# The last 16 channels in eight PSUM banks, and one set of statistics inside the first product group

## The chip, the cores and the metric

One core of a Trainium2 chip runs the kernel. TensorE (PE) multiplies, VectorE (DVE), ScalarE (ACT) and GpSimd (POOL) do the element work, SyncE (SP) issues most of the DMAs. The metric is the device time of one execution in microseconds.

## What is computed

A ConvNeXt block on 32 images of 384 channels and 28 x 28 positions in float32, followed by a channel gate:

```python
y = conv7x7_depthwise(x) + dw_b                 # per channel
mu, var = mean(y, channels), var(y, channels)   # per position
y = (y - mu) * rsqrt(var + EPS) * ln_g + ln_b
y = gelu(y @ w1 + b1)                           # 384 -> 1536
gx = sqrt(sum(y * y, positions)); nx = gx / (mean(gx, features) + EPS)
y = grn_g * (y * nx) + grn_b + y
x = x + (y @ w2 + b2)                           # 1536 -> 384
avg, mx, mn = mean(x, positions), max(x, positions), min(x, positions)
logits = concat(avg @ W1.T, grouped(mx, W2_1) * W2_2, mn @ W3.T) @ Wfc.T
out = sigmoid(logits + x)
```

## The kernel before

*The convolution.* Channels go in 48 steps `s` of eight, four pairs a step. For each channel, three matmuls (L697, L699, L701) multiply the turned image rows of all images by a banded matrix `tmat`. The result of a pair stands in one PSUM bank `pc`. VectorE turns it into `yt` (L704) and adds it to `acc`, the sum over channels (L712). ScalarE squares `yt` into `sq` (L718), and POOL adds the squares of two pairs to `ssum` (L728). Each `yt` of eight channels is stored to the scratch tensor `yd`.

*The last 16 channels.* They are done in step 47, in two halves of images (0 to 15, then 16 to 31), so that image 0 is ready earlier. The four banks `pc_half` serve eight pairs in turn. Each half adds its own share to `acc` and to its own copy of `ssum`, and is stored to `yd`: the first in whole tiles, the second in quarters from SP's and ScalarE's queues. Between the halves, image 0's last 16 channels are read back from `yd` (`load_y_part`).

*The statistics.* `finish` runs twice, once for each half of the images: mean, variance, square root, reciprocal, and a store of the reciprocal `rs` to the scratch tensor `rsd`. Its temporary tiles (`late`) lie in a buffer of the convolution's `xt` pool. From `rsd`, `load_rb(b)` brings the factors of one image to all partitions as `rb`.

*Forms.* A 3 x 6 block of operands (three channel blocks, two halves of the positions) is multiplied by a 3 x 3 block of weights with 15 products instead of 18. The operands are the forms p to x and z, made of sums of the blocks `0a` to `2b` (`FORMS`, made in `forms_up`), and three of the blocks themselves. The weights of the 15 products, `u1d`, are made during the convolution. For image 0, whose factors come too late, the products work on data that is not yet multiplied by `rs`. Its result is multiplied afterwards (`stretch`, L944). Forms q, t and u of image 0 are made by POOL before the last step, and the rest by VectorE after it (`first_image(2)`).

*The up-projection.* `up(b, hooks)` computes y for image b in two groups of two tiles each (`t2` is 0, then 2). A group runs the 15 steps of `UPSTEPS`, each for both tiles. A step is one product into a bank (A, B or C of its tile), after which the listed reads are done: a copy by ScalarE, or additions by VectorE. A bank that is written anew waits until it has been read. Weights are loaded by `load_u1` in portions of five steps into six rotating buffers in `ws`. After each product `run(hooks, (t2, step))` issues other work that was entered for that place: a step's number is twice the row's number, plus one for the second tile.

*What the hooks hold.* `within(b)` enters work for `up(b)`: for image 0 the normalization of image 1 (`normed`) and its forms, the stretches and gelu of image 0, and the loads of image 2's y (`load_y`); for image 1 the rest of image 0's work (stretch, gelu, `square`, `grn`, `scale`) and the sums of its down-projection. `beside(b)` does the same for `down(b)`.

*The down-projection.* `down(b)` runs 38 steps of six matmuls on 39 `SUMS` of y. A sum of 128 x 588 elements is one POOL instruction (L1069) into a slot of `d_room`, into a place that has become free, or over an operand that is not used again.

*Order.* A scheduler orders each engine's instructions at build time. `keep_in_program_order` puts an instruction behind the one traced before it on its engine; DMAs that SP issues count as SP's instructions. An engine runs its list in order, so one that waits holds up what stands behind it. Memory of the convolution's pools is given to later pools (`up2`, `tep`, `yp`, `xp`, `d_room`), which wait for its last readers. `before` runs `load_rb(0)`, `load_y(1)`, `up(0)`, `up(1)`, `down(0)`, then `up(2)`, `down(1)`, and so on.

Of the kernel before, what the change touches and what calls it, by code (L numbers as in the profile page):

```python
# [13 lines left out]
P = 128  # L14
# [72 lines left out]
)  # L87
NS = len(UPSTEPS)
KT = FB // 3
# [108 lines left out]
def convnext_gate_kernel(  # L198
# [24 lines left out]
    rsd = [dram.tile([P, YR], F32, name=f"rsd_{i}") for i in range(2)]  # L223
# [18 lines left out]
    fct = const.tile([P, CB, NQ, R], F32, name="fct")  # L242
    eps_t = const.tile([P, 1], F32, name="eps_t")
# [9 lines left out]
    def load_u1(t, i):  # L253
        n = len(u1_tiles) % NU1
        w = ws[:, n * UG * P : (n + 1) * UG * P].rearrange("p (g c) -> p g c", c=P)
        nc.sync.dma_start(w, u1d[t, :, i : i + UG, :])
        u1_tiles.append(w)
        return w
# [23 lines left out]
    def load_rb(b):  # L282
        if b == 0:
            rb = d_room[:, : NQD * YR].rearrange("p (q n) -> p q n", n=YR)
        else:
            rb = rbp.tile([P, NQD, YR], F32, tag="rb", name=f"rb_{b}")
        rbs[b] = rb
        base = rsd[0 if b < B0 else 1]
# [3 lines left out]
                tensor=base.tensor,  # L292
                offset=base.offset + b * YR,
# [4 lines left out]
    def load_y_part(b, yi, cb, p0, p1):  # L298
        nc.sync.dma_start(
            yi[p0:p1, cb],  # L300
            yd.rearrange("(q b) c n -> b c q n", b=B)[b, cb * P + p0 : cb * P + p1],
        )
# [25 lines left out]
    def forms_up(b, eng=nc.gpsimd, early=None):  # L328

        if b in feats:  # L330
            o, af = feats[b], early_af.pop()
            make_forms(b, eng, o, af, [d for d in FORMS if d[0] not in EARLY])
            return
        acc = accs.pop(b)
        o = feats[b] = {
            f"{k}{'ab'[h]}": acc[:, k, h * NH : (h + 1) * NH] for k in range(CB) for h in range(2)
        }
        ns = len(FORMS) - 1
        if b == 1:

            n = -(-ns * NH // (KD * NQ4))
            reserved.extend(slots[SLOTS - n :])
            del slots[SLOTS - n :]
            aft = d_room[:, (SLOTS - n) * KD * NQ4 :]
            af = [aft[:, n * NH : (n + 1) * NH] for n in range(ns)]
        else:
            af = [room_af[:, n, :] for n in range(ns)]
        if early:
            early_af.append(af)
        make_forms(b, eng, o, af, [d for d in FORMS if not early or d[0] in EARLY])  # L350

    EARLY, early_af = ("q", "t", "u"), []

    def make_forms(b, eng, o, af, todo):
        places = [d[0] for d in FORMS if d[0] != "w"]
        for name, place, in0, in1, op in todo:
            d = o[place] if name == "w" else af[places.index(name)]
            tc.keep_in_program_order(eng.tensor_tensor(d, o[in0], o[in1], op))  # L358
            o[name] = d


    with ExitStack() as one:
# [8 lines left out]
        finp = one.enter_context(tc.tile_pool(name="finp", bufs=1))  # L371
# [70 lines left out]
        ssum = finp.tile([P, SQ, YR], F32, name="ssum")  # L442
        acc = finp.tile([P, 2, N], F32, name="acc")
        dws = finp.tile([P, 1], F32, name="dws")
        lr = tp.tile([P, CB, 2], F32, name="lr")
        mcol = tp.tile([P, FB], F32, name="mcol")
        for t in (ssum, acc):
            nc.gpsimd.memset(t, 0.0)
# [224 lines left out]
        def conv(s, c2, yt, xt, b0, b1):  # L673
# [7 lines left out]
            else:  # L681

                pc = pcs.pop(0)
                pcs.append(pc)
# [21 lines left out]
            def part(v):  # L706
                if nb == B:
                    return v
                return v.rearrange("p c (j b) -> p c j b", b=B)[:, :, :, b0:b1]

            a = part(acc)
            keep(nc.vector.tensor_tensor(a, a, part(pc[:, :, :N]), ALU.add))  # L712
# [10 lines left out]
            if cy % SQ == SQ - 2:  # L723
                to, base = ssum, ssum
                if nb < B and not b0:
                    to = late["s2"]
                    base = ssum if s == NK - 2 and cy < SQ else to
                nc.gpsimd.tensor_tensor(to, base, sq, ALU.add)  # L728
# [7 lines left out]

        late = {}

        def finish(half, b0, b1):

            def part(v):
                return v.rearrange("p (j b) -> p j b", b=B)[:, :, b0:b1]

            mu0, s1, mu, va, s2, rs = (late[f"t{6 * half + i}"] for i in range(6))
            nc.vector.tensor_tensor(part(mu0), part(acc[:, 0]), part(acc[:, 1]), ALU.add)
            nc.vector.transpose(s1, mu0)
            nc.vector.tensor_reduce(
                s2, (ssum if half else late["s2"]).rearrange("p c n -> p n c"), AX.X, ALU.add
            )
            nc.vector.tensor_scalar(mu, s1, dws, 1.0 / C, ALU.add, ALU.mult)  # L750
            nc.vector.tensor_tensor(va, mu, mu, ALU.mult)
            nc.vector.scalar_tensor_tensor(va, s2, 1.0 / C, va, ALU.mult, ALU.subtract)
            nc.vector.tensor_scalar(va, va, 0.0, EPS, ALU.max, ALU.add)
            nc.scalar.activation(s2, va, AF.Sqrt)
            nc.vector.reciprocal(rs, s2)
            nc.sync.dma_start(rsd[half], rs)

        def late_tiles():

            t = new_xt(NX).rearrange("p c n -> p (c n)")  # L760
            late["s2"] = t[:, : SQ * YR].rearrange("p (c n) -> p c n", n=YR)
            for i in range(12):
# [562 lines left out]
```

## Time and profile before

| | |
|---|---|
| median of 3 runs | 3058.28 us (3057.81 to 3059.55) |
| the profiled execution | 3060.93 us |
| its span, first to last instruction | 3059.1 us |
| mean granted TensorE clock | 0.994 |
| last product of the convolution ends | 507.2 us |
| first product of up(0), up(1), down(0), up(2) | 513.3, 567.8, 613.8, 658.3 us |

The profile is of one execution. A busy time is a sum over instructions of one engine. A row of the view by stage has the busy time of each engine in one stretch of the span, the granted clock as a share of full speed, the share in which the 16 DMA engines are busy, and the rate. The chain of waits follows the last instruction back to what released each step of it: start, length, engine, tile and line. A row of a timeline names start, duration, engine, line, operation, tiles, and in brackets the idle time before it with what ended it.

### The profile page before, as it was taken

What the parts mean: (1) busy time and instruction counts of PE and PEld (TensorE: products, weight loads), DVE (VectorE), ACT (ScalarE), POOL (GpSimd) and SP (SyncE); (2) the same over time, 40 slices, a digit from 0 to 9 for tenths busy, and PEclk for the clock granted to TensorE, in tenths of its full rate; (3) what the DMA queues carried; (4) which work ended last, traced back from release to release, by engine and by line L of the source; (5) the groups of instructions that cost most, each with busy time, mean ns of one, the idle gap of its engine ahead of it and who ended that gap; (6) DMA issues with size and microseconds to landing.
All of it is one profiled execution on the core that took longest, in us unless ns stands there. A gap on an engine that the chain in (4) does not pass through costs nothing.

```text
span 3059.1 us, 43987 instructions
## 1 busy us (share of the span) xinstructions
PE 3000.1 (98%) x14435; PEld 2428.2 (79%) x14435; DVE 2038.2 (67%) x4642; ACT 1792.1 (59%) x2916; POOL 2445.7 (80%) x1822
## 2 busy tenths in 40 slices
PE   7999998999999999999999999999999999999998
PEld 7999997477777777777777777777777777777777
DVE  5766666756666666666666666666666666666665
ACT  3455554756666666666666666666666666666661
POOL 3357865599888888888888888888888888888897
PEclk9999998999999999999999999999999999999999
DMA  9899997456666666666666666666666666666646
GB/s 328 329 348 380 367 352 242 132 169 203 205 206 201 202 206 205 199 201 199 196 201 205 204 197 197 197 197 196 198 197 201 201 201 202 202 200 202 195 152 201
DMA packets 285836, 674.15 MB, mean 220 GB/s; under 512 B 30864, under 2 KB 106411, under 8 KB 279595
## 3 DMA queue, kind: packets, MB, share of 16 engines
q1 hardware_dynamic: 272644, 633.00, 62.9%
q10 hardware_dynamic: 12966, 38.34, 3.2%
q8 instruction: 118, 1.93, 0.3%
q14 instruction: 108, 0.88, 0.1%
HBM read 575.57 MB, written 95.68 MB: 219 GB/s over the span
## 4 chain that ended last, share of the span: by engine, by line
PE 87%; POOL 4%; DVE 4%; DMA 2%; ACT 1%; issue 1%; DVEq 0%; ACTq 0%; SPq 0%; POOLq 0%
PE ph_C L978 13%; PE ph_A L978 12%; PE ph_B L978 11%; PE pz_A L1108 8%; PE pz_C L1108 8%; PE pz_F L1108 7%; PE pz_D L1108 7%; PE pc L697 4%; PE pc L699 4%; PE pc L701 4%; PE pt L487 2%; PE pz_H L1108 2%; PE pz_I L1108 2%; PE pz_E L1108 2%; POOL d_room L1069 2%; DVE room L315 2%
## 5 line engine op out<-in xcount | busy, mean ns | idle before, releaser
L326 ACT ACTIVATE y<-y,fv,gsc 128x784 f32<-128x784 f32 x372 | 359.1, 1031 | 463.5 <-DVE gsc L1016 463.5
L1069 POOL TENSOR_TENSOR d_room<-y 128x588 f32<-128x588 f32 x253 | 364.2, 1441 | 288.3 <-PE pz_B L1108 192.2
L937 ACT ACTIVATE y<-y,b1f 128x784 f32<-128x784 f32 x384 | 350.3, 945 | 208.3 <-DVE y L995 178.2
L978 PE MATMUL ph_B<-room,ws 128*128 128x392 f32 x1240 | 461.9, 495 | 9.8 <-issue 6.1
L978 PE MATMUL ph_C<-room,ws 128*128 128x392 f32 x1240 | 464.7, 497 | 6.5 <-DVE y L993 2.1
L978 PE MATMUL ph_A<-room,ws 128*128 128x392 f32 x1240 | 459.6, 493 | 3.8 <-POOL room L358 2.0
L1069 POOL TENSOR_TENSOR d_room<-d_room,y 128x588 f32<-128x588 f32 x308 | 440.7, 1435 | 16.8
L978 PEld LDWEIGHTS ph_C<-room,ws 128*128 128x128 f32 x1240 | 234.5, 191 | 190.8 <-DVE y L993 27.9
L978 PEld LDWEIGHTS ph_A<-room,ws 128*128 128x128 f32 x1240 | 236.1, 191 | 177.8 <-POOL room L358 2.6
L978 PEld LDWEIGHTS ph_B<-room,ws 128*128 128x128 f32 x1240 | 236.1, 191 | 174.5 <-issue 7.2
L728 POOL TENSOR_TENSOR ssum<-ssum,sq 128x896 f32<-128x896 f32 x96 | 200.7, 2090 | 176.6 <-ACT sq L718 175.2
L950 ACT ACTIVATE junk<-y 128x784 f32<-128x784 f32 x384 | 329.1, 857 | 9.0
L1069 POOL TENSOR_TENSOR d_room<-y,d_room 128x588 f32<-128x588 f32 x214 | 306.1, 1437 | 27.2 <-PE pz_D L1108 15.8
L358 POOL TENSOR_TENSOR room<-room 128x392 f32<-128x392 f32 x303 | 303.5, 1018 | 11.9
L718 ACT ACTIVATE sq<-yt,dwb 128x224 f32<-128x224 f32 x376 | 160.5, 474 | 233.6 <-DVE yt L704 223.6
L1069 POOL TENSOR_TENSOR y<-y 128x588 f32<-128x588 f32 x180 | 258.7, 1437 | 7.1
L991 DVE TENSOR_TENSOR y<-y,ph_B 128x392 f32<-128x392 f32 x256 | 137.3, 557 | 160.4 <-ACT y L937 119.3
L989 DVE TENSOR_TENSOR y<-y,ph_C 128x392 f32<-128x392 f32 x384 | 212.7, 562 | 26.2 <-PE ph_C L978 1.4
L704 DVE STREAM_TRANSPOSE yt<-pc 128x448 f32<-128x448 f32 x184 | 119.3, 648 | 148.5 <-PE pc L701 100.6
L697 PE MATMUL pc<-xt,tmat 128*128 128x224 f32 x736 | 201.8, 356 | 4.6 <-ACT xt L498 4.1
L1108 PE MATMUL pz_A<-d_room,u 128*128 128x196 f32 x1050 | 203.0, 330 | 0.1
L1108 PEld LDWEIGHTS pz_A<-d_room,u 128*128 128x128 f32 x1050 | 178.7, 190 | 7.7 <-POOL d_room L1069 0.4
(264 smaller groups left out, 6371.2 us busy)
## 6 DMA issues: line engine op xcount, KB each, us to landing
u<-u2d SPq DMA_DIRECT2D x487, 384.0 KB, 3.9
ws<-u1d SPq DMA_DIRECT2D x384, 320.0 KB, 3.0
tmat<-fs SPq DMA_DIRECT2D x47, 1420.0 KB, 11.0
ws<-u2d SPq DMA_DIRECT2D x121, 384.0 KB, 3.9
yi<-yd SPq DMA_DIRECT2D x95, 448.0 KB, 6.1
yd<-yt SPq DMA_DIRECT2D x47, 896.0 KB, 6.6
x<-in_x SPq DMA_DIRECT2D x32, 1176.0 KB, 5.6
out<-x ACTq DMA_DIRECT2D x31, 1176.0 KB, 9.6
```

The source lines that it names most:

```text
L326: eng.activation(out, in_, AF.Identity, bias=add, scale=mul)
L358: tc.keep_in_program_order(eng.tensor_tensor(d, o[in0], o[in1], op))
L697: keep(nc.tensor.matmul(po, t[:, c, P : 2 * P], xc, start=True, stop=False))
L718: nc.scalar.activation(sq[:, cy % SQ + ci], yt[:, cy + ci], AF.Square, bias=dwb[:, cc + ci : cc + ci + 1], scale=1.0,)
L728: nc.gpsimd.tensor_tensor(to, base, sq, ALU.add)
L937: ins = nc.scalar.activation(y, y, AF.Gelu, bias=b1f[:, f : f + 1], scale=1.0)
L950: ins = nc.scalar.activation(junk, ys[b][:, f, :], AF.Square, accum_out=ssqs[b][:, f : f + 1])
L978: nc.tensor.matmul(banks[t, bk][:, :NH], wts[t][:, i % UG, :], o[opnd], start=(first == 1), stop=True, skip_group_check=True,)
L989: nc.vector.tensor_tensor(d, d, p, ALU.add)
L991: nc.vector.tensor_tensor(d, d, p, ALU.subtract)
L1069: nc.gpsimd.tensor_tensor(d[0], o[a][0], o[c][0], ALU.add if sign == "+" else ALU.subtract)
L1108: nc.tensor.matmul(pz[:, :NQ4], wt[:, i % UD, t, :], o[opnd][0][:, t, :], start=(first and t == 0), stop=(t == KD - 1), skip_group_check=True,
```

## The change

1. The last 16 channels stand in eight banks, two pools of three and one and one of four, so that a pair keeps its bank through both halves. The first half is turned, stored and read back for image 0 as before. In the second half a bank holds all images, so the tile is turned and stored whole, and `acc`, `sq` and `ssum` are updated once.
2. `finish` runs once, in three parts. Part 0 stands ahead of `up(0)`, parts 1 and 2 are entered at steps 13 and 17 of its first group. Its temporary tiles lie in image 0's y buffer; `acc` and `ssum` lie in a tile `stats` of their own, which also takes the place of the unused output of `square`. `load_rb(0)` and `load_y(1)` follow part 2.
3. The first group of image 0 runs `FIRST_UP`, an order in which the products w, 1a, 0b, 0a, t, q and u stand first, with a fourth bank D. Form w of image 0 gets a place in `ws`. POOL makes all forms of image 0: q, t, u, w early, p, r, s within the second half, v, x, z after it.
4. Weight loads for image 0 are pinned. All reads of image 0 and its first group's products are pinned.
5. The y pool and the bank pool are split into two pools each, used in turn.
6. Other work of images 0 and 1 moves: stretch, gelu, square, `normed(1)`, image 1's forms and `load_y(2)` within image 0's second group; `grn` and the scales within image 1's second group.
7. Of image 0's sums, those with a remaining count of one modulo four are VectorE's: ten of 39.

```diff
+FIRST_UP = (
+    ("w", "A", 1, (("A", "copy", "E"),)),
+    ("1a", "B", 1, (("B", "rsub", "E"),)),
+    ("0b", "A", 0, (("A", "negated", "1b"),)),
+    ("0a", "B", 0, (("B", "negated", "0a"),)),
+    ("t", "C", 1, (("C", "add", "E"),)),
+    ("q", "A", 0, (("A", "plus", "0b"),)),
+    ("u", "B", 0, (("B", "minus", "1a"),)),
+    ("p", "D", 1, (("D", "copy", "2b"),)),
+    ("s", "C", 1, (("C", "add", "0a"),)),
+    ("x", "A", 1, (("A", "copy", "2a"),)),
+    ("r", "D", 0, (("D", "sub", "2a"), ("D", "sub", "0a"), ("D", "add", "0b"))),
+    ("2a", "C", 0, (("C", "add", "2a"),)),
+    ("v", "A", 0, (("A", "sub", "2b"), ("A", "sub", "1b"), ("A", "add", "1a"))),
+    ("z", "C", 1, (("C", "add", "2b"), ("C", "add", "1b"))),
+    ("2b", "D", 1, (("D", "add", "2b"),)),
+)
...
-    def load_u1(t, i):
+    def load_u1(t, i, pin=False):
...
-        nc.sync.dma_start(w, u1d[t, :, i : i + UG, :])
+        ins = nc.sync.dma_start(w, u1d[t, :, i : i + UG, :])
+        if pin:
+            tc.keep_in_program_order(ins)
...
-            a = part(acc)
-            keep(nc.vector.tensor_tensor(a, a, part(pc[:, :, :N]), ALU.add))
+            if b1 < B:
+                return
+            keep(nc.vector.tensor_tensor(acc, acc, pc[:, :, :N], ALU.add))
...
+                for i in (UG, 2 * UG, 0):
+                    for t in range(2):
+                        first_u1[t, i // UG] = load_u1(t, i)
...
+                            keep(nc.sync.dma_start(yd[:, ch, :], y2[i]))
+                        if b1 == B and n == PAIRS:
+                            first_image(2)
+                        if b1 == B and n == PAIRS + 1:
+                            forms_up(0, ("p", "r", "s"))
...
+            steps = [(x[0],) + x[2:] for x in UPSTEPS]
+            if b == 0 and t2 == 0:
+                steps = FIRST_UP
+            for i, (opnd, bk, first, acts) in enumerate(steps):
                 for t in (t2, t2 + 1):
-                    if i % UG == 0:
-                        wts[t] = first_u1.pop((t, i), None) or load_u1(t, i)
+                    g, gi = divmod(PLACE[opnd], UG)
+                    if (t, g) not in wts:
+                        wts[t, g] = first_u1.pop((t, g), None) or load_u1(t, g * UG, b == 0)
...
+    def finish(part):
+        keep = tc.keep_in_program_order
+        tmp = yis[0].rearrange("p k q n -> p (k q n)")
+        mu0, s1, mu, va, s2, rs = (tmp[:, i * YR : (i + 1) * YR] for i in range(6))
+        if part == 0:
+            keep(nc.vector.tensor_tensor(mu0, acc[:, 0], acc[:, 1], ALU.add))
+            keep(nc.vector.transpose(s1, mu0))
+            keep(nc.vector.tensor_scalar(mu, s1, dws, 1.0 / C, ALU.add, ALU.mult))
+            keep(nc.vector.tensor_tensor(va, mu, mu, ALU.mult))
+            for n in (SQ // 2, 1):
+                to = ssum[:, :n] if n > 1 else s2.unsqueeze(1)
+                keep(nc.gpsimd.tensor_tensor(to, ssum[:, :n], ssum[:, n : 2 * n], ALU.add))
+            forms_up(0, ("v", "x", "z"))
+        elif part == 1:
+            keep(nc.vector.scalar_tensor_tensor(va, s2, 1.0 / C, va, ALU.mult, ALU.subtract))
+            keep(nc.vector.tensor_scalar(va, va, 0.0, EPS, ALU.max, ALU.add))
+            keep(nc.scalar.activation(s2, va, AF.Sqrt))
+        else:
+            keep(nc.vector.reciprocal(rs, s2))
+            keep(nc.sync.dma_start(rsd, rs))
+            load_rb(0)
+            if B > 1:
+                load_y(1)
...
+            eng = nc.vector if b == 0 and len(todo) % 4 == 1 else nc.gpsimd
...
         if b == 0:
+            at((0, 13), finish, 1)
+            at((0, 17), finish, 2)
+            for m in range(HF):
+                at((2, 2 * m), stretch, m, nc.gpsimd)
+                at((2, 5 + 4 * m), gelu, b, m)
+                at((2, 7 + 4 * m), square, b, m)
             if B > 1:
-                at((0, 20), normed, 1)
-                at((0, 24), forms_up, 1)
-            for m in range(HF):
-                at((2, 4 * m), stretch, m, nc.gpsimd)
+                for cb in range(CB):
+                    at((2, 7 + 4 * cb), normed, 1, (cb,))
+                at((2, 16), forms_up, 1)
             if B > 2:
-                at((2, 0), load_y, 2)
+                at((2, 20), load_y, 2)
         elif b == 1:
             for m in range(HF):
                 at((0, 2 * m), stretch, HF + m, (V, nc.gpsimd)[m % 2])
-                at((0, 6 + 2 * m), gelu, p, HF + m)
-                at((0, 17 + m), square, p, HF + m)
-            at((0, 23), grn, p)
+                at((0, 6 + 3 * m), gelu, p, HF + m)
+                at((0, 8 + 3 * m), square, p, HF + m)
+            at((2, 3), grn, p)
             for i, f in enumerate(order):
-                at((0, 24) if i < 6 else (2, 0), scale, p, f, V if i % 3 else A)
-            at((0, 26), sums, p)
-            at((2, 0), sums, p)
-            at((2, 12), sums, p)
+                at((2, 4 + i), scale, p, f, V if i % 2 else A)
+            for i in range(6, 30, 2):
+                at((2, i), sums, p)
```

## The prediction

> **What bounds the kernel now.** I read the page first (engine totals, 40 slices), then a table by stage, then the chain of waits and SP's queue in the stage that the change rewrites.
>
> ```profile
> PE 3000.1 (98%) x14435; PEld 2428.2 (79%) x14435; DVE 2038.2 (67%) x4642; ACT 1792.1 (59%) x2916; POOL 2445.7 (80%) x1822
> PE   7999998999999999999999999999999999999998
> ...
> 504.00:507.00 3.00, 3.00 (x31) 3.00 (x30) 3.00 (x6) 1.79 (x6) 2.92 (x2) 1.00 1.03 141
> 507.00:513.30 6.30, 0.21 (x2) 0.04 (x1) 6.30 (x10) 3.09 (x8) 4.78 (x3) 0.85 0.60 103
> 513.30:526.60 13.30, 7.70 (x12) 3.23 (x12) 9.42 (x16) 1.33 (x4) 0.00 (x0) 0.63 0.78 247
> 613.50:658.20 44.70, 40.37 (x232) 37.93 (x231) 22.25 (x69) 21.33 (x30) 43.45 (x33) 1.00 0.69 225
> ```
>
> The columns are window and length, then PE, PEld, DVE, ACT and POOL busy with counts, granted clock, DMA share, GB/s. TensorE bounds the kernel nearly everywhere; nothing gained on another engine counts outside its holes. The largest hole lies where the convolution passes to the first products (507 to 527): TensorE works 8 of 19 us, at 0.85 and then 0.63 of its clock. The last row is the first down-projection: POOL is 97% busy there and TensorE is not. The chain of waits names the owner of the first hole:
>
> ```profile
> 508.88 1.43 DVE xt L751
> 510.31 2.15 DVE room L790
> ...
> 519.08 1.46 DVE xt L755
> ...
> 521.43 1.47 DVE xt L755
> 522.92 2.97 DMA rsd<-xt
> 526.05 0.51 ACT y L985
> 526.60 2.98 PE ph_B L978 x4
> ```
>
> VectorE works through statistics and image 0's forms, rsd is stored, and only when that has landed does ScalarE empty the first bank (the store reads memory that the y tiles take over).
>
> The work itself: two tiles' step is 1.32 us in the chain, so 60 products are 39.5 us; 38 down steps of 0.995 us are 37.8. Against that stand, by the timeline, 507.2 to 567.8 for up(0) (60.6, excess 21.1), to 613.8 for up(1) (46.0, excess 6.5), to 658.3 for down(0) (44.5, excess 6.7), and 2.0 of waiting for a form in up(2) at 663. The change can touch these 36.3 us; image 2 onward keeps its code, and its bank and y rotations work out the same with two pools of half the size.
>
> [...]work stopped at 507.2, the 1.5 us rows read 0.50 by 512, and after the restart at 526.6 the clock is full only from about 532. Here that cost (2.98-1.32)+(2.55-1.32), about 2.9 us. [...]rb lands after 5.9 to 8.4 us, the 8.4 behind three yi loads. [...]a VectorE form takes 0.48 us alone (three in 1.43)[...].
>
> **The change, part by part.**
>
> *Banks and statistics.* All 16 channels stand in eight banks, so the bank wait at 496.5 (0.4 us) goes: last convolution product at 506.8. Sixteen SQUAREs (0.43), four POOL additions (2.09) and the first half's acc additions go; acc of the second half grows from 0.35 to 0.58. Four more memsets (0.24) lie in VectorE idle time. Second-half stores become two on SP instead of eight on SP and ScalarE's queue. They overwrite channels that image 0's small load reads, so they wait for it (landing 2.2 us after its issue at about 504.3); nothing needs them before image 1's y, 15 us later. The first six weight loads now stand on SP before the first half; in before they were issued from 479 to 490 already, and their memory is freed by the same POOL work (487), so nothing moves. Form w takes the place of the fifth down-weight buffer, whose load was issued at 496.2: it now waits for up(0)'s last product w and is first used at step 8 of down(0), some 50 us on. One rsd store and one set of vector work on the second half go with their 3 us. Only one set of finish instructions remains, now with short POOL folds for the two 1.7 us reductions.
>
> *Group one.* Seven products of the new order need only forms made early, on channels already loaded. I walk the queues. VectorE: 1.23 us a pair, pair 4 not before yt_a's store has landed (504.2), pair 7 done 509.1, finish(0) 1.6 more. ScalarE: image 0's last block (0.93) at 506.6, then three pairs of SQUAREs, so free at 510.1; its first copy then starts. Product 0b, reached at 509.4, waits for it: about 1.1 us. POOL: addition 5 from 508.4, p r s to 513.6, addition 7 to 515.7, folds to 517.5, v x z to 520.6 (1.02 each). TensorE with 1.32 a step reaches s at 518.6 and x at 520.0; x is made at 519.6. VectorE reads PSUM 15 times a tile instead of 11, three times in a row for r and for v: about 1 us for z. Sum: 506.8 + 19.8 + 2.1 = 528.7. Before, the same 30 products ended at 543.7; 15 us won here.
>
> *Where it is late next.* Group two's weights. Six buffers exist, and the first two are in use to product z. The new loads are pinned behind what was traced before them on SP: rsd, rb 0, three y loads of image 1, rb 1. All of those wait for rsd. Its reciprocal follows s on VectorE: 520.7 + 1.5 = 522.2, landing 3.1 later, 525.4. Image 1's y cannot come sooner, as it takes the memory where rs stands. In before, y came at 513 to 521 and the weights had 11 us.
>
> ```profile
> 523.35 0.38 SPq L289 DMA_DIRECT2D rb<-rsd  x1
> 526.04 0.37 SPq L289 DMA_DIRECT2D d_room<-rsd  x1
> 530.92 8.15 SPq L256 DMA_DIRECT2D ws<-u1d  x4
> ...
> 543.19 1.56 SPq L299 DMA_DIRECT2D yi<-yd  x3
> 544.80 0.88 SPq L289 DMA_DIRECT2D rb<-rsd  x1
> 545.78 22.56 SPq L256 DMA_DIRECT2D ws<-u1d  x8
> ```
>
> From the 1.5 us rows, two rb moved at about 165 to 198 GB/s (2.6 us each) and y at about 300 (4.6 for three). If y stands ahead: 525.4 + 1.6 + 2.6 + 4.6 + 2.6 + two weights of 1 us = 538.5. If only both rb do: 534. The order isn't decided by the code; I take 536.5: 7.8 us idle, and[...] a half clock after it (2.5[...]). Bounds: 2 us if the queue is empty, 12 if other loads stand in it.
>
> *Group two* has a second such place: image 2's y and rb are traced between the last weight loads of the two tiles, at step 20, and wait for normed(1), the third part of which follows step 15. With TensorE at 551 that is done near 550 to 552; y, rb and the weights land 9.5 later, some 7.1 us after the product wants them; half clock again, 2.5. Bounds 1 and 12. Hence up(1) begins at 528.7 + 7.8 + 2.5 + 19.8 + 7.1 + 2.5 = 568.4: 0.6 late instead of 18 early. Moved past on the queues: normed(1) goes from group one to group two on VectorE, behind whose reads it now stands in order; image 2's four loads go from the first to the eleventh step on SP; SQUARE and gelu of image 0 interleave with ScalarE's copies (4.7 + 12 us of 19.8). Behind a waiting weight on TensorE stand only products; the stretches (six of 1.93 on POOL), normed (three of 1.03) and image 1's forms (10.3) are hidden in that same time. Uncovered, they would cost the last forms, about 2 us.
>
> *up(1).* The normalization moves behind step 1 of group two, the 12 scales to one a step, 6 each on VectorE and ScalarE. ScalarE's first group holds 16.7 us of 19.8. VectorE in the second has 22 reads of 0.52, 6 scales of 0.89 and up to 3 sums: 20 us. I leave 3.5 of the 6.5 excess: 3.0 won.
>
> *down(0).* Ten of 39 sums go to VectorE: POOL 29 x 1.44 = 41.8 instead of 56.2. A VectorE sum is not in the trace; a form scaled by size (0.48 x 588/392) is 0.73.[...] Lower bound: nothing won; upper 14. Step by step the sums then trail TensorE by up to 2.2 us, so excess 2.5 for 6.7: 4.2 won. Image 2's forms come earlier: 1.6 of the 2.0 won. On VectorE, the reads of step banks queue behind a waiting sum.
>
> Sum: -0.6 + 3.0 + 4.2 + 1.6 = 8.2 us. The profiled execution is 3060.93 (span 3059.1), giving 3052.7; the median of the runs, 3058.28, is 2.65 lower, giving **3050**. Changes in idle time of other engines count nothing.
>
> **Rivals.** *B, the weights are in time*: waits of 2 and 2 without half clock. 5.8 + 5.1 + 5.0 more: 24 won, 3034. For it: the loads before landed without any wait of TensorE on them. Against it: they were then ahead of y, with 11 us to spare. *C, slower: VectorE's sums.* Place: up(1)'s second group and down(0). A sum waits for its POOL operand and the bank reads behind it wait too, then TensorE. At a POOL sum (1.44) held for each of the ten, 14.4 lost: 3064. It decides the sign from 0.82 us each. For it: POOL is 97% busy, and VectorE has no slack in that group. Against it: eight banks give TensorE some lead, and most sums are old when asked for. *D, no change*: image 0's x (1.18 MB) also falls in front of both weight loads, 3.9 us at 300 GB/s, twice: 0.4 won, 3058.
>
> **How the numbers follow.** A (forecast) 0.44, B 0.24, C 0.17, D 0.15. About 0.2% (6.1 us) separates change from none. A lies in 3041 to 3060: 0.30 faster, 0.11 same, 0.03 slower. B is faster, 0.24. C: 0.02, 0.03, 0.12. D: 0.04, 0.09, 0.02. Together 0.60, 0.23, 0.17. The range 3033 to 3064 leaves out about 0.10 of B below and 0.08 of C above.
>
> **What would show it.** Right: group one follows the convolution within 1 us and ends near 529; TensorE then waits for a weight load, with the clock at 0.5; again before product 0a of the last tile; up(1) starts near 568; down(0) lasts 40 us. Wrong: no wait on ws (B), VectorE waiting for POOL with TensorE behind (C), a first product after 511 (a whole-pool wait on the old banks), or a difference after image 2.

## The result, and the profile after

| | before | after |
|---|---|---|
| median of 20 runs each, taken together | 3059.63 us (3054.98 to 3062.66) | 3062.87 us (3059.84 to 3068.62) |
| ratio | | 1.0013, 95% interval 1.0007 to 1.0020 |
| profiled execution; its span | 3060.93; 3059.1 us | 3061.04; 3059.3 us |

The change makes the kernel about 0.13% slower. The two profiled executions differ by only 0.1 us, which hides what happened: in the profile after, the convolution ends at 502.4 us instead of 507.2, and from there to the first product of down(1) it takes 198.1 us instead of 192.8. The readings below count from the end of the convolution. All stage times are single profiles.

| us | end of convolution to down(0) | down(0) | up(2) | sum |
|---|---|---|---|---|
| before | 106.6 | 44.5 | 41.8 | 192.8 |
| after | 102.3 | 56.3 | 39.5 | 198.1 |

The page of the kernel after (engine totals, and TensorE's 40 slices) looks like the one before:

```profile
PE 3001.7 (98%) x14435; PEld 2432.2 (80%) x14435; DVE 2033.5 (66%) x4637; ACT 1787.0 (58%) x2901; POOL 2428.9 (79%) x1814
PE   8999998989999999999999999999999999999998
```

Only the ninth slice (612 to 688 us), now an 8, hints at it. The view by stage of the kernel after shows it (window, length, busy PE, PEld, DVE, ACT, POOL with counts, granted clock, DMA share, GB/s):

```profile
505.40:524.80 19.40, 17.56 (x52) 9.33 (x50) 16.84 (x31) 4.13 (x10) 9.98 (x9) 1.00 0.44 138
524.80:532.58 7.78, 0.03 (x1) 0.00 (x0) 3.16 (x7) 0.00 (x0) 5.98 (x4) 0.69 1.04 363
532.58:604.70 72.12, 66.02 (x183) 35.71 (x184) 53.11 (x88) 53.53 (x91) 34.68 (x25) 0.94 0.42 140
604.70:661.00 56.30, 44.82 (x232) 43.11 (x231) 30.23 (x76) 24.36 (x36) 48.13 (x36) 0.85 0.54 178
661.00:700.50 39.50, 39.50 (x122) 22.80 (x122) 29.00 (x54) 23.76 (x43) 29.27 (x22) 1.00 0.31 102
```

The big hole after the convolution is gone, one of 7.8 us is left, and up(2) runs without a gap. But the first down-projection lasts 56.3 us, with POOL no longer full (48.1 of 56.3) and the clock at 0.85. SP's queue of the kernel after shows why the 7.8 us hole is there (start, time that the row's issues span, line, tiles):

```profile
518.50 0.32 SPq L1002 DMA_DIRECT2D rsd<-yi  x1
520.22 0.37 SPq L313 DMA_DIRECT2D d_room<-rsd  x1
520.64 2.57 SPq L323 DMA_DIRECT2D yi<-yd  x3
523.25 0.83 SPq L313 DMA_DIRECT2D rb<-rsd  x1
524.18 4.67 SPq L279 DMA_DIRECT2D ws<-u1d  x5
```

The weights stand last. And the timeline of TensorE in the kernel after shows its three waits of over 4 us (the bracket is the idle time ahead of the row and what ended it; the rows after a long wait are twice as long as the others of their kind, 1.48 or 1.16 us):

```profile
532.58 2.98 PE L956 MATMUL ph_B<-room,ws 128*128 128x392 f32 x4 [7.75 <-DMA ws<-u1d]
...
609.67 1.23 PE L1114 MATMUL pz_F<-d_room,u 128*128 128x196 f32 x6
616.61 2.30 PE L1114 MATMUL pz_A<-d_room,u 128*128 128x196 f32 x6 [5.71 <-DVE x L1130]
...
637.89 2.30 PE L1114 MATMUL pz_A<-d_room,ws 128*128 128x196 f32 x6 [4.10 <-issue]
```

In down(0) TensorE did six steps, banks A to F, and its seventh, which takes bank A again, stood until VectorE had read A. VectorE's timeline in the same place:

```profile
607.60 3.90 DVE L1077 TENSOR_TENSOR d_room<-y 128x588 f32<-128x588 f32 x2 [2.14 <-POOL y L1077]
611.43 0.35 DVE L1130 TENSOR_TENSOR x<-x,pz_A 128x196 f32<-128x196 f32 x1
614.21 1.98 DVE L1077 TENSOR_TENSOR y<-d_room,y 128x588 f32<-128x588 f32 x1 [2.44 <-POOL d_room L1077]
616.12 0.34 DVE L1130 TENSOR_TENSOR x<-x,pz_A 128x196 f32<-128x196 f32 x1
...
636.48 0.77 DVE L1077 TENSOR_TENSOR d_room<-y,d_room 128x588 f32<-128x588 f32 x1 [3.67 <-POOL y L1077]
...
637.44 0.35 DVE L1130 TENSOR_TENSOR x<-x,pz_A 128x196 f32<-128x196 f32 x1
```

The first product in bank A is read twice, at 611.43 and 616.12, and ahead of each read (L1130) stands a sum (L1077) that waited for POOL. The row at 637.44 also tells what the "issue" of 4.10 us was: bank A was read at 637.44 and TensorE went on at 637.89. The list of waits of the kernel after, from 604.7 to 661 us, adds them up (us in total, times, longest):

```profile
DVE d_room L1077 <- POOL y L1077: 8.5, 4, 3.7
...
DVE y L1077 <- POOL d_room L1077: 2.4, 1, 2.4
...
DVE d_room L1077 <- POOL d_room L1077: 2.1, 1, 2.1
```

```profile
PE pz_A L1114 <- DVE x L1130: 6.1, 2, 5.7
PE pz_A L1114 <- issue: 4.1, 1, 4.1
PE pz_C L1114 <- DVE x L1130: 1.3, 1, 1.3
```

VectorE waited 13.0 us for POOL, and TensorE 11.5 us for VectorE. The seven sums themselves took 11.4 us of VectorE: five lay beside a sum of POOL and took 1.95 to 1.98 us each, the other two 0.77. After the two long waits six steps ran wholly or partly at half clock (granted clock 0.50 from 613.05 to 623.29 us and from 636.95 to 643.77); by the distances of their starts they cost 5.9 us more than 0.995 each. 37.8 us (38 steps) + 11.5 + 5.9 is 55.2 of the 56.3 us.

### The profile page after: what moved, and what is told of

Same layout as the page of the kernel before. It is cut to its first block, busy times and chain, and to the rows that moved or that the text cites. A ratio compares the mean times of both kernels' runs of the same rounds, so it can differ in the third digit from the quotient of the medians.

```text
span 3059.3 us, 43821 instructions
## 1 busy us (share of the span) xinstructions
PE 3001.7 (98%) x14435; PEld 2432.2 (80%) x14435; DVE 2033.5 (66%) x4637; ACT 1787.0 (58%) x2901; POOL 2428.9 (79%) x1814
## 4 chain that ended last, share of the span: by engine, by line
PE 92%; DVE 3%; POOL 2%; DMA 1%; issue 1%; ACT 1%; SPq 0%; ACTq 0%; DVEq 0%; POOLq 0%
PE ph_C L956 13%; PE ph_A L956 12%; PE ph_B L956 12%; PE pz_A L1114 8%; PE pz_C L1114 8%; PE pz_F L1114 7%; PE pz_D L1114 7%; PE pc L712 5%; PE pc L714 4%; PE pc L716 4%; PE pt L504 2%; PE pz_H L1114 2%; PE pz_I L1114 2%; PE pz_E L1114 2%; POOL d_room L1077 1%; DVE room L339 1%
## 5 line engine op out<-in xcount | busy, mean ns | idle before, releaser
L1077 POOL TENSOR_TENSOR d_room<-y 128x588 f32<-128x588 f32 x247 | 355.5, 1443 | 305.8 <-PE pz_B L1114 220.3
L1077 POOL TENSOR_TENSOR d_room<-d_room,y 128x588 f32<-128x588 f32 x307 | 440.2, 1438 | 17.6 <-DVE d_room L1077 0.9
L956 PEld LDWEIGHTS ph_B<-room,ws 128*128 128x128 f32 x1232 | 233.9, 191 | 176.1 <-DMA ws<-u1d 11.4
L735 POOL TENSOR_TENSOR stats<-stats,sq 128x896 f32<-128x896 f32 x96 | 200.8, 2092 | 180.4 <-ACT sq L729 176.9
L924 ACT ACTIVATE stats<-y 128x784 f32<-128x784 f32 x384 | 329.3, 858 | 9.1
L1077 POOL TENSOR_TENSOR d_room<-y,d_room 128x588 f32<-128x588 f32 x212 | 304.2, 1441 | 27.9 <-PE pz_D L1114 15.9
L1077 POOL TENSOR_TENSOR y<-y 128x588 f32<-128x588 f32 x180 | 258.9, 1438 | 6.4
L969 DVE TENSOR_TENSOR y<-y,ph_C 128x392 f32<-128x392 f32 x386 | 213.7, 562 | 24.8
```

The lines of the kernel that those rows point to most:

```text
L735: ins = nc.gpsimd.tensor_tensor(ssum, ssum, sq, ALU.add)
L924: ins = nc.scalar.activation(stats[:, :NT], ys[b][:, f, :], AF.Square, accum_out=ssqs[b][:, f : f + 1])
L956: ins = nc.tensor.matmul(banks[t, bk][:, :NH], wts[t, g][:, gi, :], o[opnd], start=(first == 1), stop=True, skip_group_check=True,)
L969: ins = nc.vector.tensor_tensor(d, d, p, ALU.add)
L1077: eng.tensor_tensor(d[0], o[a][0], o[c][0], ALU.add if sign == "+" else ALU.subtract)
```

## The experiments

Theory H: the ten sums on VectorE hold up the bank reads behind them in VectorE's queue, and that turns a gain into a loss. The rivals: the sums come late whoever makes them; or the late weights, the other new wait, are the loss. Each kernel was profiled and timed in turn with the kernel before on one chip; a ratio is to that. "Lead" is the time from POOL's first sum for image 0 to the first product of down(0).

| kernel | to down(0) | down(0) | up(2) | sum | lead | median us | ratio, 95% interval |
|---|---|---|---|---|---|---|---|
| before | 106.6 | 44.5 | 41.8 | 192.8 | 19.1 | | 1 |
| after | 102.3 | 56.3 | 39.5 | 198.1 | 15.4 | 3062.87 | 1.0013 (1.0007 to 1.0020) |
| a_pool_sums | 100.8 | 49.4 | 41.8 | 192.0 | 13.5 | 3059.40 | 0.9996 (0.9988 to 1.0004) |
| b_dve_sums | 110.9 | 51.2 | 39.5 | 201.7 | | 3068.53 | 1.0025 (1.0016 to 1.0034) |
| a_old_sums | 100.9 | 52.9 | 39.5 | 193.2 | | 3059.39 | 0.9995 (0.9987 to 1.0003) |
| a_act_copies | 100.8 | 53.2 | 39.5 | 193.5 | | 3061.77 | 0.9999 (0.9991 to 1.0007) |
| a_y12_later | 98.8 | 55.0 | 39.5 | 193.3 | | 3059.35 | 0.9999 (0.9991 to 1.0007) |
| a_y12_later_pool | 97.8 | 49.4 | 44.3 | 191.5 | 13.6 | 3058.81 | 0.9988 (0.9981 to 0.9995) |
| a_grn_early_pool | 105.1 | 47.1 | 41.8 | 194.0 | 17.4 | 3061.80 | 0.9995 (0.9987 to 1.0003) |
| a_y12_grn_pool | 98.9 | 47.1 | 44.4 | 190.4 | 17.4 | 3055.89 | 0.9981 (0.9975 to 0.9988) |
| a_all_n2 | 90.8 | 50.9 | 40.1 | 181.8 | 17.4 | 3049.64 | 0.9965 (0.9952 to 0.9977) |
| a_all_n2_w | 92.3 | 49.2 | 41.8 | 183.3 | 17.4 | 3050.16 | 0.9962 (0.9949 to 0.9976) |
| b_n2 | 105.3 | 46.7 | 44.3 | 196.3 | 19.1 | 3064.34 | 1.0010 (1.0003 to 1.0016) |
| a_pool_n2 | 99.7 | 51.5 | 41.8 | 193.0 | 13.5 | 3064.01 | 1.0005 (0.9997 to 1.0013) |

### The sums on VectorE: taken away, and put into the kernel before

**a_pool_sums**, the kernel after with all 39 sums on POOL:

```diff
-            eng = nc.vector if b == 0 and len(todo) % 4 == 1 else nc.gpsimd
+            eng = nc.gpsimd
```

> The changed kernel with all 39 sums of image 0 on POOL again; nothing else differs. Theory H (VectorE's sums hold the bank reads behind them): in down(0) the waits of TensorE for VectorE's reads (5.7, 1.3, 0.4 and 4.1 us) and the half clock after two of them go. POOL then has 39 x 1.44 = 56.2 us from about 589 on, so down(0) ends near 651 and up(2) waits for image 2's forms until about 655: some 6 us faster than the changed kernel, about 3057 where that has 3063. Rival P (POOL is late whoever does the sums, since the down-projection starts 4 us sooner after the convolution): down(0) stays at 56 us or grows by up to 7, no gain or slower.

**b_dve_sums**, the kernel before with the ten sums on VectorE:

```diff
-                nc.gpsimd.tensor_tensor(
+                (nc.vector if b == 0 and len(todo) % 4 == 1 else nc.gpsimd).tensor_tensor(
```

> The kernel before with the ten VectorE sums alone. Theory H: down(0) grows from 44.5 by 8 to 12 us, with TensorE waiting for VectorE's reads of x, total about 3069. Rival P: POOL is relieved by 7 to 14 us, down(0) falls to 40 to 42 us and the 2 us wait in up(2) goes, total about 3054.

The first takes 6.1 us from the stages, the second adds 8.9 to them. The times follow: the interval of a_pool_sums lies below that of the kernel after, and the kernel before became 0.25% slower by this one line. TensorE's waits of a_pool_sums in down(0) are now on POOL:

```profile
611.80 1.60 PE L1114 MATMUL pz_F<-d_room,u 128*128 128x196 f32 x6 [3.27 <-POOL d_room L1077]
621.65 1.26 PE L1114 MATMUL pz_D<-y,u 128*128 128x196 f32 x6 [0.63 <-POOL y L1077]
627.55 1.26 PE L1114 MATMUL pz_E<-y,u 128*128 128x196 f32 x6 [1.66 <-POOL y L1077]
637.51 1.26 PE L1114 MATMUL pz_H<-d_room,u 128*128 128x196 f32 x6 [1.51 <-POOL d_room L1077]
```

and those of b_dve_sums have the pattern of the kernel after, VectorE first and then TensorE:

```profile
625.14 1.98 DVE L1069 TENSOR_TENSOR d_room<-y 128x588 f32<-128x588 f32 x1 [0.79 <-POOL y L1069]
...
644.13 0.77 DVE L1069 TENSOR_TENSOR d_room<-y,d_room 128x588 f32<-128x588 f32 x1 [3.75 <-POOL y L1069]
```

```profile
627.80 2.30 PE L1108 MATMUL pz_C<-d_room,u 128*128 128x196 f32 x6 [2.35 <-DVE x L1124]
...
645.54 2.30 PE L1108 MATMUL pz_A<-d_room,ws 128*128 128x196 f32 x6 [4.11 <-issue]
```

In b_dve_sums down(0) grew by 6.7 us, less than the 8 to 12 expected. Another 4.3 were lost ahead of it, where a sum at 601.25 waited 2.84 us for POOL and TensorE then 3.96 us (603.76) for a bank read behind that sum; up(2) won 2.3. So the total came out as expected, its parts did not. That the ten sums cost time is shown from both sides. What a_pool_sums leaves open is why it isn't faster than before, although it reaches down(0) 5.8 us sooner. The column "lead" answers: image 0's normalization and scales are entered later in up(1), POOL starts its sums 13.5 instead of 19.1 us ahead of down(0), and TensorE waits the difference away there (49.4 against 44.5).

### Which sums, and whose queue

**a_old_sums**, ten other sums on VectorE, chosen as those whose operands are oldest in the list:

```diff
+    OLD = "s5 s14 s15 s18 s23 s26 s27 s30 s33 s35".split()
...
-            eng = nc.vector if b == 0 and len(todo) % 4 == 1 else nc.gpsimd
+            eng = nc.vector if b == 0 and name in OLD else nc.gpsimd
```

> The changed kernel with ten other sums on VectorE, none of whose operands is the sum that POOL made just before (s5 s14 s15 s18 s23 s26 s27 s30 s33 s35). Theory H in the form that the wait for a POOL operand does the holding: VectorE's waits for POOL in down(0) shrink from about 13 us to under 4, down(0) takes 41 to 45 us instead of 56, total 10 us less than the changed kernel. Theory H in the form that any VectorE sum holds (its own time,[...] or the place it writes): down(0) stays at 52 to 56, total within 3 us of the changed kernel.

Down(0) took 52.9 us, 3.4 less than in the kernel after and not the 41 to 45 of the first form. VectorE still waited 12.7 us for POOL there, not under 4. Its timelines of VectorE and of TensorE:

```profile
623.05 0.77 DVE L1077 TENSOR_TENSOR y<-y 128x588 f32<-128x588 f32 x1 [7.10 <-POOL y L1077]
```

```profile
626.37 2.30 PE L1114 MATMUL pz_F<-d_room,ws 128*128 128x196 f32 x6 [6.46 <-DVE x L1130]
```

This sum, s23, waited 7.1 us for POOL, although POOL makes neither of its operands (the blocks 0d and 2d of y). What is left is the place in y that it writes over: the wait ended with POOL's sum s22 (621.60 to 623.02), which stands just ahead of it in the list and also works in y. So the place that is written can hold a queue as an operand can, and age in the list doesn't tell.

**a_act_copies** puts a ScalarE copy of the first operand in the place of each of the ten sums; the second operand is left out of them.

```diff
+            if b == 0 and len(todo) % 4 == 1:
+                ins = nc.scalar.activation(d[0], o[a][0], AF.Identity)
+            else:
+                ins = nc.gpsimd.tensor_tensor(
```

> The kernel after with VectorE's ten sums replaced by ten ScalarE copies of their first operand (the second operand is left out), in the same places of program order, waiting for the same POOL results and POOL waiting for them. Theory H (the bank reads that stand behind a waiting sum on VectorE hold TensorE): TensorE's waits on VectorE in the first down-projection (5.7 us at 616.6, 4.1 at 637.9) go, and since POOL is still relieved of ten sums the stretch from its first product to the first product of up(2) is 39 to 42 us instead of 56.3, and convolution to down(1) 184 to 189 instead of 198. Rival (the sums come late whoever makes them, as they wait on POOL's chain; VectorE's reads play no part): TensorE waits as long for the copies, and the stretch stays above 52 us.

Up to its 23rd step TensorE had no wait of 0.3 us: that step began 22.1 us after the first (625.42 and 603.27), in the kernel after 40.1 (644.84 and 604.70). Up to there ScalarE's copies had themselves waited 4.6 us for POOL (2.61, 0.54 and 1.46), and TensorE did not wait for them. So the rival falls: results that waited for POOL were in time, and what had held TensorE was VectorE's queue. The run does not tell how much of that was the waiting and how much the length of the sums: a copy took ScalarE 0.69 us also beside POOL, a sum took VectorE up to 1.98. By the timeline above, 13.0 us were waits and about 6 the lengthening (five sums at 1.2 us more than 0.77). Yet the stretch lasted 53.2 us, as here ScalarE's queue was held (timelines of ScalarE, then of TensorE):

```profile
632.18 0.69 ACT L1076 ACTIVATE d_room<-y 128x588 f32<-128x588 f32 x1 [2.85 <-POOL y L1078]
...
637.00 0.21 ACT L1011 ACTIVATE gx<-ssq 128x12 f32<-128x12 f32 x1
```

```profile
637.47 0.59 PE L1015 MATMUL pg<-gs,ones_f 128*128 128x1 f32 x2 [10.89 <-DVE gs L1013]
```

Image 1's squares stood behind copies that waited for POOL, the root `gx` came at 637.00, and TensorE's own queue had the small product `pg` of image 1's normalization ahead of the next steps. The hold had only changed its engine. My 39 to 42 us were wrong because I had considered only what stands behind the sums on VectorE.

### The late weights

**a_y12_later** moves the loads of images 1 and 2 behind the weight loads:

```diff
-            if B > 1:
-                load_y(1)
...
+                at((2, 1), load_y, 1)
...
-                at((2, 20), load_y, 2)
+                at((2, 21), load_y, 2)
```

> The changed kernel with image 1's y traced after the first two weight loads of group two, and image 2's y after the last one. Theory W (the weights are late because of what stands ahead on SP[...]): the first wait of TensorE falls from 7.75 to about 3 us and the half clock after it goes (2.9), the second (2.0, with products of up(1) pulled ahead of it) goes; down(0) starts 6 to 10 us sooner than its 102.2 us after the convolution. Theory H says that down(0) still takes 53 to 57 us, so the total falls by what up(0) won, 6 to 10 us. Rival: the first wait is the memory of the weight buffers, in use to product z, and the total falls by under 3.

The first wait went from 7.75 to 4.24 us, and the second on weights is gone. One of image 1's three y loads still went ahead of the weights (at 521.47, the weights at 523.72), and no run takes away the remaining 4 us. Most of the gain came back as a wait of 4.72 us on VectorE, with a half clock after it (2.95 us for four products that take 1.48), so that 3.5 us are won to down(0) and not 6 to 10. The timelines of VectorE and TensorE:

```profile
555.53 4.68 DVE L919 TENSOR_TENSOR y<-y,d_room 128x784 f32<-128x784 f32 x2
560.14 3.56 DVE L339 SCALAR_TENSOR_TENSOR room<-yi,cv,rb 128x784 f32<-128x784 f32 x2
```

```profile
565.26 2.95 PE L956 MATMUL ph_C<-d_room,ws 128*128 128x392 f32 x4 [4.72 <-DVE y L969]
```

Image 2's normalization (L339), ready earlier, now lies beside stretches of image 0 (L919), in front of bank reads (L969).

In time this run is level with a_pool_sums (3059.35 and 3059.40 us, on one chip): taking away either delay brings the kernel back to the time of the one before. The six variants of the kernel after with 192.0 to 194.0 us by stage lie at 0.9995 to 1.0005, with intervals that overlap, and can't be told apart by their times. So the late weights have a share in the loss too. But the prediction had priced them (7.8 + 2.5 + 7.1 + 2.5 = 19.9 us), whereas it had put the sums down as a gain; and b_dve_sums, which has no late weights of this kind, is slower by the sums alone.

**a_y12_later_pool** has both edits, loads and sums:

> The kernel after with two edits: the loads of images 1 and 2 moved behind the weight loads in SP's queue, and all 39 sums on POOL. If the gains add (first edit 4.8 us of the stretch from convolution to down(1), second 6.1, by their own runs), that stretch is 187 to 188 us instead of 198.1, and the time some 5 us under the kernel before (ratio 0.998). Rival (with sums on POOL, POOL's queue decides when down(0) can go, and an earlier start of it is only waited away there): conv to down(0) 98 to 99, but down(0) with up(2) 93 instead of 91, total 191 to 192, ratio 0.9995 to 1.0.

The rival was nearly right: the sum is 191.5. The median is 0.12% below before, the first one that is clearly lower.

### Making up the lead, and what stood in VectorE's queue

**a_grn_early_pool** and **a_y12_grn_pool** enter image 0's normalization and its scales four steps earlier, and its sums three, with all sums on POOL; the second has the later loads too.

```diff
-            at((2, 3), grn, p)
+            at((0, 25), grn, p)
             for i, f in enumerate(order):
-                at((2, 4 + i), scale, p, f, V if i % 2 else A)
+                at((0, 26 + i) if i < 4 else (2, i - 4), scale, p, f, V if i % 2 else A)
-            for i in range(6, 30, 2):
+            for i in range(0, 30, 2):
```

> The kernel after with all 39 sums on POOL, and image 0's normalization and its 12 scales entered three steps earlier in up(1), the first of them in its first group, so that POOL can begin the sums about 4 us sooner. If POOL's queue of sums decides down(0), its waits there (3.3, 0.6, 1.7, 1.5 and 2.0 us in up(2)) shrink by 4 us in all: convolution to down(1) 188 us instead of 192.0. Rival (ScalarE is back to back in that part of up(1) with squares, gelu and table loads, so the normalization cannot come sooner, or its place in the queue holds copies of banks): sums begin at the same time, 192 or more.

> All three edits together: loads of images 1 and 2 behind the weights, sums on POOL, normalization and scales of image 0 earlier. If the gains add: convolution to down(1) 183 to 185 us, 8 to 10 under the kernel before, time near 3052 (ratio 0.997). If POOL's queue or ScalarE decides instead: 189 to 192, ratio 0.999 to 1.0.

The lead grew by 3.8 us in both and down(0) shrank to 47.1, 2.3 less; down(0) follows POOL's start, if not by the whole of it. The first run lost it again before down(0) (105.1 instead of 100.8): 1.4 us in new waits on ScalarE's bank copies (0.99 and 0.39), which stand among the scales, and some 2.8 at 575.21, where TensorE waited 2.02 us for a bank read behind stretches (0.69 in a_pool_sums) and then ran at about half clock (2.49 us for four products at 577.93 that take 1.48 elsewhere). Whether the edit causes this second part isn't shown. The second run is 0.19% faster than before, by less than I had put.

**a_all_n2** keeps image 2's three normalizations in program order, that is in down(0); **a_all_n2_w** also image 1's y loads.

```diff
-            if b == 1:
+            if b in (1, 2):
                 tc.keep_in_program_order(ins)
```

> a_y12_grn_pool with image 2's three normalizations by VectorE kept in program order, that is in the first down-projection instead of between the stretches at the end of up(0). If the 5.2 us wait of TensorE there (568.75, on VectorE) comes from these instructions standing ahead of the bank reads in VectorE's queue, it shrinks to under 2 us, and convolution to down(0) falls from 98.9 to about 95; down(0) is unchanged at 47, convolution to down(1) about 187, time near 3053. Rival (VectorE's stretches alone hold the reads, or the normalizations beside POOL lengthen POOL's sums in down(0)): the wait stays over 4 us, or down(0) grows by 3 or more, total 190 or above.

> a_all_n2 with image 1's y loads also kept in program order, so that none of them goes ahead of the two late weight loads. If TensorE's first wait for weights (4.7 us) is made up of what moves ahead of them, one y load (1.5 us) goes from in front: wait 3 to 3.5 us, time about 1.5 us lower than a_all_n2, near 3051. Rival (the weights are bound by the release of their buffer and the transfer's own latency): wait unchanged at 4.5 us or more.

The 5.2 us wait fell to 0.44 (timelines of TensorE, first of a_y12_grn_pool, then of a_all_n2):

```profile
568.75 2.95 PE L956 MATMUL ph_C<-d_room,ws 128*128 128x392 f32 x4 [5.20 <-DVE y L969]
```

```profile
562.40 0.93 PE L956 MATMUL ph_C<-d_room,ws 128*128 128x392 f32 x2 [0.44 <-DVE y L969]
```

By stage, first a_y12_grn_pool, then a_all_n2, from the end of the convolution to down(0):

```profile
505.80:604.70 98.90, 86.23 (x243) 47.02 (x242) 76.25 (x125) 62.28 (x112) 55.62 (x39) 0.93 0.52 171
```

```profile
504.90:595.80 90.90, 83.31 (x243) 45.49 (x242) 70.10 (x122) 62.31 (x112) 54.95 (x39) 0.98 0.53 179
```

8.0 us less there, of which 2.9 is TensorE's busy time (86.23 us at a mean clock of 0.93, 83.31 at 0.98), and up(2) is 4.3 less (a wait of 0.33 us instead of 2.05 on its form). Down(0) is 3.8 longer, with the normalizations beside POOL's sums there (VectorE takes 1.95 to 1.99 us for each), so this part of the rival came true as well. This version beats both kernels, by 0.35% against before. The last edit moved one rb ahead instead of one y load, and the wait on weights was 5.25 us, not shorter: its expectation missed, and its time can't be told from that of a_all_n2.

**b_n2** and **a_pool_n2** make the same edit in the kernel before and in a_pool_sums:

> The kernel before with image 2's three normalizations by VectorE kept in program order (in the first down-projection instead of at 559.8 to 575 us). If this order alone is worth the 8 us that it brought on top of the other edits, whatever the rest of the kernel: convolution to down(1) 185 us instead of 192.8, ratio 0.9975. If it pays only where VectorE stands close behind TensorE: the kernel before has only 0.7 us of TensorE's waits near that place, so 190 to 193, ratio 0.999 to 1.0. The end of the convolution, untouched, also shows what this kernel's early part does from run to run (507.2 and 506.6 so far).

> The kernel after with all 39 sums on POOL and image 2's normalizations kept in program order, the loads and image 0's normalization left as they are. There these stand at 557 to 576 us and cost VectorE 3.1 us, none beside POOL. If the 8.6 us came from the shared cover (loads behind the weights put the normalizations beside POOL's stretches), this brings under 3 us: convolution to down(1) 189 to 192 instead of 192.0, ratio 0.999. If it stands by itself: 184.

Alone it brings nothing: 0.10% slower on the kernel before, where by stage it is 3.5 us longer and outside both of the expected ranges, and no gain on a_pool_sums (193.0 instead of 192.0). It paid on top of the later loads and the earlier scales of image 0. The likely reason is that the later loads had put the normalizations beside POOL's stretches (two of them took 5.15 us at 562.03 in a_y12_grn_pool, where one alone takes 1.03). Which of the two other edits it needs was not separated.

## Why the prediction was wrong, step by step

It gave 3050 us and 0.60 to faster. The kernel became slower, in the way of rival C (0.17).

- *Group one, 15 us won*: right. Predicted 21.9 us from the end of the convolution to the end of the group (528.7 less 506.8), measured 22.4. Its small waits were others: not 1.1 us for ScalarE's copy at product 0b, but 1.48 for VectorE's read at product 0a (508.17).
- *First late weights, 7.8 us and a half clock of 2.5*: right in kind, and 7.75 and 2.9 by measurement (granted clock 0.50 from 527.72 to 537.96 us); that the wait agrees so closely is luck. It was the middle of two orders of the queue, and the trace has the worse one, all three y loads and both rb ahead of the weights. For that order the terms give 538.8 (not 538.5, as written), so a wait of about 10.
- *Second late weights, 7.1 and 2.5*: too large. They landed 8.4 us after their issue at 549.3, but the build had set four products of up(1) ahead (551.46 and 554.21), so 2.0 us were left and a half clock of 1.8 (granted clock 0.50 from 558.44 to 561.85 us). This also goes against rival B, which put waits of 2 us without a half clock.
- *To down(0)*: 102.3 us. The terms gave 104.6 (106.6 less 3.0 for up(1), plus 1.0, which is the 0.6 of the sum and the 0.4 by which the convolution was to end sooner). The second weights were 5.8 better than their term (9.6 less 3.8), so group two or up(1) was worse than its own by some 3. One place is a wait of 1.97 us at 597.40 on a bank read: ahead of that read VectorE's queue had two sums (1.44 us) and then two scales, which took 3.51 us beside POOL where three took 1.88 alone. So it is only in part rival C's place.
- *down(0)*, the step that failed: "Ten of 39 sums go to VectorE: POOL 29 x 1.44 = 41.8 instead of 56.2", "excess 2.5 for 6.7: 4.2 won". It became 11.8 longer. I counted what POOL is relieved of and priced the lower bound at "nothing won", though the same paragraph ends with the reads that queue behind a waiting sum. What the runs show in its place: POOL was relieved (busy for 48.1 of 56.3 us), but VectorE's queue waited 13.0 us for POOL, and TensorE lost 11.5 us behind it and 5.9 at half clock. Only rival C put a price on that line, 14.4 us from ten waits of one POOL sum each. Its 3064 is near the measured 3062.87, but partly by luck: six sums waited and not ten, up to 3.67 us each, and the half clock was not in its sum.
- *The argument against C*, "eight banks give TensorE some lead, and most sums are old when asked for": both halves were wrong. The steps take bank A again at the seventh of them, so the lead is at most six steps, 6 us, and six of the seven sums that VectorE did in down(0) had to wait for POOL. In the timeline of the kernel after, no read of a bank passed a waiting sum in 13.0 us of waits.
- *VectorE beside POOL*: a sum took VectorE 0.77 us alone (0.73 estimated) and 1.98 beside POOL, and POOL's took 1.83 to 1.96 there instead of 1.43. In the kernel before, the forms of image 0 on VectorE (0.50 to 0.56 us each) don't show it, as POOL was idle beside nearly all of them; L751 does, with 1.50 us beside POOL at 508.81 and 0.39 alone at 514.93.
- *up(2), 1.6 won*: right, 2.3. Image 2's forms start at 638.72 instead of 653.60.
- *A difference ahead of the change*: not foreseen beyond 0.4 us. The convolution ended at 506.6 to 507.2 in the three profiles of the kernel before and its two variants, and at 502.3 to 506.3 in the eleven of the kernel after and its variants, 2.3 us earlier in the mean. That fits what the medians give (3.2 us slower with 5.3 lost in the stages). In the first two profiles it arises at 60 to 80 us, where TensorE was busy for 14.6 of 20 us before and 18.1 after, with the DMA engines 96% busy in both; whether the change causes it stays open.

The sum of the stages was to fall by 7.8 us (8.2 less the 0.4) and rose by 5.3. Without the ten sums it fell by 0.8 in a_pool_sums: the 5.8 us won ahead of down(0) were nearly all waited away at POOL's sums, whose lead the later normalization had shortened by 5.6 us.

## What to carry to other kernels

Before moving work from a full engine to one with slack, list what stands behind it in the new engine's queue and who waits for that: an operation that must wait for another engine (for an operand, or for the place that it writes) holds up every bank read behind it, as it did here in kernels with sums on VectorE (TensorE waited up to 5.71 us behind one in the kernel after, 4.11 in b_dve_sums, 6.46 in a_old_sums). The lead that the banks gave here was the distance to the next use of the same bank in the order of steps (six steps, 6 us), not their number. And when one stage is shortened, check that its successor's supplier starts sooner too: here 5.8 us won ahead of down(0) came back as 4.9 in it, and it took four moves together (sums back on POOL, loads behind the weights, image 0's normalization and scales earlier, image 2's normalization out of VectorE's way) to be 0.35% faster than before; without the last it was 0.19%.

## What was not expected of the hardware

A wait of the same 2.0 us halved TensorE's clock in one profile and not in another. In b_n2:

```profile
663.56 1.78 PE L978 MATMUL ph_A<-room,ws 128*128 128x392 f32 x4 [2.02 <-POOL room L358]
665.13 2.82 PE L978 MATMUL ph_B<-room,ws 128*128 128x392 f32 x4
667.75 1.73 PE L978 MATMUL ph_C<-room,ws 128*128 128x392 f32 x4
```

and in the kernel before:

```profile
663.07 1.58 PE L978 MATMUL ph_A<-room,ws 128*128 128x392 f32 x4 [2.01 <-POOL room L358]
```

The product after it took 2.82 instead of 1.48 us in b_n2, and up(2) 44.3 instead of 41.8. The granted clock was 0.72 from 664 to 670 us in b_n2, and 1.00 from 663 to 670 in the kernel before. The kernel after has a third such wait. From 495 to 715 us the views by stage of the two main profiles show the granted clock only at 1.00 and 0.50, at 0.50 in these stretches:

| profile | granted clock 0.50 (us) | lengths of these stretches | lengths of those between them, at 1.00 |
|---|---|---|---|
| before | 511.46 to 521.70, 525.12 to 531.95 | 10.24, 6.83 | 3.41 |
| after | 527.72 to 537.96, 558.44 to 561.85, 613.05 to 623.29, 636.95 to 643.77 | 10.24, 3.41, 10.24, 6.83 | 20.48, 51.20, 13.65 |

In both, each length is a whole multiple of 3.413 us (1, 2, 3, 4, 6 and 15 times), within rounding. By an estimate from these changes, counted on in steps of 3.413 us, the waits of these two profiles lie like this:

| profile | wait of TensorE | steps that it falls into | idle in each | clock in the step after |
|---|---|---|---|---|
| before | 661.06 to 663.07 | 658.24 to 661.65, and to 665.07 | 0.59, 1.41 us | 1.00, 1.00 |
| after | 555.76 to 557.79 | 555.03 to 558.44 | 2.03 us | 0.50, until 561.85 |

By this count the wait that lay whole in one step was followed by half clock, and the one split over two was not. These are two waits, which show no rule; what set the clock in b_n2 is not shown. The shortest of these stretches at half clock, 3.41 us, costs 1.7 us by its length, and the six microseconds at 0.72 in b_n2 cost as much. So a difference of some 2 us between single profiles in the table may be that alone, and the ratios decide.
